# A constant moved ahead of the SBUF rings, and the output projections of four batches in a row in every second unit

## The chip, the cores and the metric

The kernel runs on one core of one Trainium2 chip, as one launch. The metric is device microseconds (us) of that core. The chip's engines have the names of the profile: PE (TensorE, the matmuls), PEld (its weight loads), DVE (VectorE), ACT (ScalarE), POOL (GpSimd) and SP (SyncE, which issues nearly all DMAs here).

## The reference

Four blocks change a residual `x` of 8 batches, 128 rows and 512 columns. Each adds tanh(gate) times its result to `x`; the first is by far the largest:

```python
x = x + tanh(g_xattn[0]) * L0_xattn(layernorm(x), ctx, mask, bias, ln_w, w_q, w_k, w_v, w_out)
x = x + tanh(g_ffn[0])   * L0_ffn(layernorm(x), 4-bit weights)
x = x + tanh(g_xattn[1]) * L1_xattn(layernorm(x), ctx, ...)
x = x + tanh(g_ffn[1])   * L1_ffn(layernorm(x), ...)
# L0_xattn: 32 heads of 128
score = einsum('bqhd,bkhd->bhqk', rmsnorm(x) @ w_q.T, ctx @ w_k.T) + position_bias
attn  = einsum('bhqk,bkhd->bqhd', softmax(masked score), ctx @ w_v.T)
out   = hidden + attn.reshape(b, q, 32 * 128) @ w_out.T
```

The last line is what the change touches: the projection of the heads' outputs, 4,096 wide, to 512 columns.

## The kernel before

**Number format.** Most products are made of three matmuls: each operand is split into a rounded high part and the low rest, and `product` (L172) adds high times high (L178), high times low (L179) and low times high (L182) in one PSUM bank. The operands have the type float32r, in which a column passes PE once; scores and attention (L691, L755) are plain float32, which the profile shows as two records for each matmul. A matmul has a stationary operand of 128 columns, loaded by PEld, and a moving one of up to 512 columns that streams past it.

**Stages.** First (to some 350 us) all keys and queries are projected and stored in DRAM. Then 64 *units* follow: unit u is one head and one half of the batches (four of them), four units to a pair of heads. At last (from some 740 us) the remaining projections and the other three blocks. In `unit(u)` (L1055) the program writes, in this order: output projections, steps of the value projection (`make_values`, in blocks of seven products that hold a PSUM bank `mm` over six of them), the attention of unit u-4 (`attend`, L743), another output projection, more value steps, the masks on POOL (`add_masks`), the scores of unit u with their softmax (`scores`, L683), then the loads, stores and the split of the next output weights (`split_wo`, L358).

**An output projection.** `project_out(p, b)` (L779) makes the 128 by 512 block `pso` of one batch b and one pair of heads p with six matmuls, three for each head: stationary are parts of the attention's output `a` (ring `page`), moving the parts `wo_h` and `wo_l` of the output weights (ring `wo`). After that one DVE instruction of L776 adds it times the gate to `xs[b]` and so frees its bank. A pair of heads has eight of these, n = 8p + b counts them all, 128 together. The PSUM ring `mm` has three banks, for `pso` and for the first accumulator `c1` of the value steps.

**Which unit takes which.** In unit u from 6 on, n = 2(u-6) is projected at the unit's beginning and n+1 after the attention. The last twelve are written out in `ending()` (L1406), two to four at a time.

**What sets the order.** The framework's planner orders the instructions of each engine when the program is built: it walks its own estimate of the time, prefers what is written earlier, and takes what is written later where the earlier isn't ready. It works on single instructions, so that six matmuls of a projection can be parted by those of a value step. `behind(name)` (L140) queues each instruction of a block, on the engine of the marked one, behind the instruction that has last been marked with that name; `mark` sets it. Within the units PE's order is the planner's, but for such edges; in the first and the last stage it is that of the program text (`in_order`).

**Where tiles lie.** SBUF tiles of the pool `sb` are laid out in the order in which their tags first occur, each rounded up to 32 bytes. The first 1,152 bytes are the framework's. Behind them stand the rings `raw` (7 tiles of 2,048 bytes) and `wo` (8), `pT` (2), the eight rows `xs`, `gates_in` (16 bytes, so 32), then the rings `moved` and `bias`, `ident`, `neghalf` (32 bytes, L411), small tiles, and the rings `v`, `page`, `kq` and `s`. So `raw`, `wo`, `pT` and `xs` begin at multiples of 64 bytes (`wo` at 15,488), and `moved`, `bias`, `ident`, `v`, `page`, `kq` and `s` at 32 bytes past such a multiple (`page` at 92,320).

Of the kernel before, what the change touches and what calls it, by code (L numbers as in the profile page):

```python
# [17 lines left out]
P = 128  # L18
NB = 8
# [47 lines left out]
def kernel(  # L67
# [37 lines left out]
    nc = tc.nc  # L105
# [6 lines left out]
    def keep(shape, name, dtype=F32):  # L112
        return sb.tile(shape, dtype, tag=name, name=name)
# [4 lines left out]
    def page(shape, name, dtype=F32R):  # L118


        return slot(shape, "page", name, dtype)

    def wide_row(tag, name, dtype=F32):
        return slot([P, D], tag, name, dtype)

    def ptile(shape, tag, name):
        return psum.tile(shape, F32, tag=tag, name=name, bufs=BANKS[tag])

    def wide(t):

        return t.bitcast(F32)
# [4 lines left out]
    def mark(name, inst):  # L136
        marks[name] = inst.ins

    @contextmanager
    def behind(*names):  # L140
        with ExitStack() as stack:
            for name in names:
                stack.enter_context(tc.issue_after(marks[name]))
            yield
# [27 lines left out]
    def product(out, terms, start=True, stop=True, **more):  # L172


        n = len(terms)
        for i, ((lh, ll), (rh, rl)) in enumerate(terms):
            first, last = start and i == 0, stop and i == n - 1
            nc.tensor.matmul(out, lhsT=lh, rhs=rh, start=first, stop=False, **more)  # L178
            nc.tensor.matmul(out, lhsT=lh, rhs=rl, start=False, stop=False, **more)  # L179
            mark(  # L180
                "product",
                nc.tensor.matmul(out, lhsT=ll, rhs=rh, start=False, stop=last, **more),  # L182
            )
# [191 lines left out]
    def load_half(h, inner):  # L375
        if inner == 0:
            raws[f"wk_{h}"] = slot([P, NDC, P], "raw", f"raw_wk_{h}")
        dcs = slice(inner * HK, inner * HK + HK)
        nc.sync.dma_start(out=raws[f"wk_{h}"][:, dcs], in_=wk[:, h, dcs])

    for inner in range(2):
        for half in range(2):
            for dc in range(inner * HK, inner * HK + HK):
                if half == 0 and dc == inner * HK:
                    load_half(0, inner)
                t = wide_row("wo", f"cxraw{half}{dc}")
                queue = nc.scalar if dc == half == 0 else nc.sync
                queue.dma_start(out=t, in_=ctxT[:, dc, half * HALF * P : (half + 1) * HALF * P])
                cx_raw[half, dc] = t
                if half == 0 and dc == inner * HK:  # L390
                    load_half(1, inner)
# [16 lines left out]
    idle = ptile([P, P], "av", "idle")  # L408
    for _ in range(WARMING):
        nc.tensor.matmul(idle, lhsT=ident, rhs=ident, start=True, stop=True)  # L410
    neghalf = keep([P, NB], "neghalf")  # L411
    nc.gpsimd.memset(neghalf, -0.5)

    tg = keep([P, 4], "tg")
# [217 lines left out]
    def by_block(t):  # L632

        return t.rearrange("p b (n k) -> p n b k", k=Q32)
# [31 lines left out]
    def where(u):  # L666

        p, r = divmod(u, 4)
        half, i = divmod(r, 2)
        return 2 * p + i, half  # L670

    def add_masks(u):

        h, half = where(u)
        s = slot([P, NQ, HALF, Q32], "s", f"s_{u}")
        bias = biases[h // 2][:, h % 2, :].rearrange("p (n k) -> p n k", k=Q32)
        with behind(*(f"norm{u - 2}",) * (u > 1)):
            nc.gpsimd.tensor_tensor(  # L678
                s, mneg[:, half], bias.unsqueeze(2).to_broadcast([P, NQ, HALF, Q32]), ALU.add
            )  # L680
        return s

    def scores(u, s):  # L683
        _, half = where(u)
        q, k = fetched.pop(("queries", u)), fetched.pop(("keys", u))
        bs = slice(half * HALF, (half + 1) * HALF)
        ps = ptile([P, HALF, P], "sc", f"sc_{u}")
        for j in range(HALF):
            cols = bass.ts(j, P)
            with behind(*("product",) * (u < SHORT)):  # L690
                nc.tensor.matmul(  # L691
                    ps[:, j, :], lhsT=q[:, cols], rhs=k[:, cols], start=True, stop=True
                )
        nc.vector.tensor_tensor(s, by_block(ps), s, ALU.add)  # L694
        nm = small.tile([P, HALF], F32, tag="nm", name=f"nm_{u}")
        mark(
            "max",
            nc.vector.tensor_reduce(  # L698
                nm, s.rearrange("p n b k -> p b n k"), AX.XY, ALU.max, negate=True
            ),  # L700
        )
        if u > 2:
            with behind("max"):
                transpose_probs(u - 3)
        sm = small.tile([P, HALF], F32, tag="sm", name=f"sm_{u}")
        for j in range(HALF):
            one = s[:, :, j, :]
            e = nc.scalar.activation(  # L708
                one, one, AF.Exp, bias=nm[:, j : j + 1], accum_out=sm[:, j : j + 1]
            )  # L710
        mark("exp", e)
        rs = small.tile([P, HALF], F32, tag="rs", name=f"rs_{u}")
        nc.vector.reciprocal(rs, sm)
        mark("rs", nc.vector.tensor_tensor(rs, rs, anykey[:, bs], ALU.mult))  # L714
        factors = rs.unsqueeze(1).unsqueeze(3).to_broadcast([P, NQ, HALF, Q32])
        mark(f"norm{u}", nc.gpsimd.tensor_tensor(s, s, factors, ALU.mult))  # L716
        probs[u] = s
# [19 lines left out]
    def transpose_probs(u):  # L737

        t = slot([P, HALF, P], "pT", f"pT_{u}")
        nc.vector.transpose(by_block(t), probs[u])  # L740
        probs[u] = t

    def attend(u):  # L743
        h, half = where(u)
        p, i = divmod(h, 2)
        pT = probs.pop(u)
        if i == 0:
            attns[p, half] = page([P, 2, 2, HALF, P], f"a_{p}_{half}")
        a = attns[p, half][:, i]
        ah, al = a[:, 0], a[:, 1]  # L750
        cols = bass.ts(i, P)
        av = ptile([P, HALF, P], "av", f"av_{u}")
        for b in range(HALF):
            v = values_of[p, half, b // 2][:, b % 2, :]
            nc.tensor.matmul(av[:, b, :], lhsT=v[:, cols], rhs=pT[:, b, :], start=True, stop=True)  # L755
        mark("a", nc.scalar.copy(ah, av))  # L756
        mark("al", nc.vector.tensor_tensor(al, av, wide(ah), ALU.subtract))  # L757

# [13 lines left out]
    def add_to_x(b, ps, factor, then=None):  # L772

        out = {} if then is None else {"accum_out": col(f"sum{then}", b)}
        mark(
            "x", nc.vector.scalar_tensor_tensor(xs[b], ps, factor, xs[b], ALU.mult, ALU.add, **out)  # L776
        )

    def project_out(p, b):  # L779
        half, j = divmod(b, HALF)  # L780
        ps = ptile([P, D], "mm", f"pso_{p}_{b}")
        product(
            ps,
            [
                (tuple(attns[p, half][:, i, part, j, :] for part in range(2)), wos[2 * p + i])
                for i in range(2)
            ],
        )
        add_to_x(b, ps, tgx0, "h1" if p == NP - 1 else None)
# [242 lines left out]
    def make_values(n):  # L1032
        nonlocal made
        while made < n:
            next(value_work, None)
            made += 1
# [18 lines left out]
    def unit(u):  # L1055
        p, r = divmod(u, 4)

        n = 2 * (u - OUT_LAG)

        goal = 14 + int(1.74 * (u - 3)) + min(AHEAD, u - 3, NU - 1 - u) if u > 3 else 0  # L1060
        if n >= 0:
            project_out(*divmod(n, NB))
        make_values((made + goal + 1) // 2)
        if u >= LAG:
            attend(u - LAG)
        if n >= 0:
            project_out(*divmod(n + 1, NB))
        make_values(goal)
        s = add_masks(u)
        for _ in range({0: 2, 1: 2, 2: 1, 3: 1, 4: 1}.get(u, 0)):  # L1070
            next(last_keys)
        scores(u, s)

        reads_first = 0 < u < SHORT or u == NU - 1
        if reads_first:
            move_probs(u - 1)
        with behind(*("moved",) * (0 < u < SHORT)):
            store_probs(u)
        if u and not reads_first:
            with behind("through"):  # L1080
                move_probs(u - 1)
        with behind("through" if u < SHORT else "moved"):
            loads(u + 1)
        if r < 2 and p:
            with behind("exp"):
                split_wo(2 * p - 2 + r)
        if u == NU - 1:
            with behind("exp"):
                split_wo(H - 2)

    make_values(7)
    unit(0)
    make_values(11)
    unit(1)
# [433 lines left out]
```

## Time and profile before

| | us |
|---|---|
| median of 3 runs (lowest to highest) | 911.24 (910.36 to 912.07) |
| the profiled execution's own time | 910.93 |
| its span, first to last instruction | 909.1 |
| PE busy in the span | 902.0 (99%) |
| DVE, ACT, POOL busy | 673.2 (74%), 503.1 (55%), 460.1 (51%) |
| granted PE clock | full |

A row of the profile's groups names the line, the engine, the operation, the tile written and those read, the shapes and how many there were; behind the bar stand the busy time in us, the mean duration of one in ns, and the engine's idle time just ahead of such instructions with what ended most of it. A row of the timeline gives the start and the duration in us of one instruction or of a few alike in a row. Matmuls overlap in the pipeline, so what a matmul takes of PE's time is read from one start to the next and not from its duration.

### The profile page before, as it was taken

What the parts mean: (1) busy time and instruction counts of PE and PEld (TensorE: products, weight loads), DVE (VectorE), ACT (ScalarE), POOL (GpSimd) and SP (SyncE); (2) the same over time, 40 slices, a digit from 0 to 9 for tenths busy, and PEclk for the clock granted to TensorE, in tenths of its full rate; (3) what the DMA queues carried; (4) which work ended last, traced back from release to release, by engine and by line L of the source; (5) the groups of instructions that cost most, each with busy time, mean ns of one, the idle gap of its engine ahead of it and who ended that gap; (6) DMA issues with size and microseconds to landing.
All of it is one profiled execution on the core that took longest, in us unless ns stands there. A gap on an engine that the chain in (4) does not pass through costs nothing.

```text
span 909.1 us, 16426 instructions
## 1 busy us (share of the span) xinstructions
PE 902.0 (99%) x5381; PEld 798.5 (88%) x5381; DVE 673.2 (74%) x1353; ACT 503.1 (55%) x1426; POOL 460.1 (51%) x513
## 2 busy tenths in 40 slices
PE   9999999999999999999999999999999999999998
PEld 7888888888888899999999999999999998888897
DVE  7888778788899866777677668666686877565587
ACT  6666565667555555544536345453554534587862
POOL 2355534124322436747748557583766844265441
PEclk9999999999999999999999999999999999999999
DMA  7754477889875956577484775766767566714001
GB/s 255 255 166 159 151 213 230 292 279 286 276 235 198 308 185 197 170 205 230 143 239 152 197 222 154 217 180 192 215 167 222 163 185 180 295 47 143 1 24 71
DMA packets 125222, 174.99 MB, mean 192 GB/s; under 512 B 17104, under 2 KB 54736, under 8 KB 124112
## 3 DMA queue, kind: packets, MB, share of 16 engines
q1 hardware_dynamic: 124992, 173.68, 61.0%
q8 instruction: 42, 0.69, 0.3%
q14 instruction: 44, 0.36, 0.1%
q10 hardware_dynamic: 144, 0.26, 0.1%
HBM read 109.86 MB, written 64.03 MB: 191 GB/s over the span
## 4 chain that ended last, share of the span: by engine, by line
PE 89%; DVE 3%; POOL 2%; DMA 2%; ACT 2%; issue 1%; SPq 0%; DVEq 0%; ACTq 0%; POOLq 0%
PE c_v L178 6%; PE c_v L182 6%; PE c_v L179 6%; PE pso L182 6%; PE pso L178 6%; PE sc L691 6%; PE pso L179 6%; PE av L755 6%; PE c_q L178 6%; PE c_q L179 6%; PE c_q L182 6%; PE c_k L178 4%; PE c_k L182 4%; PE c_k L179 4%; ACT h L1149 1%; DMA cxraw<-in_cxT_dram 1%
## 5 line engine op out<-in xcount | busy, mean ns | idle before, releaser
L708 ACT ACTIVATE s<-s,nm 128x128 f32<-128x128 f32 x256 | 99.8, 392 | 78.2 <-DVE nm L698 54.0
L776 DVE SCALAR_TENSOR_TENSOR x<-pso,tg,x 128x512 f32<-128x512 f32 x128 | 93.5, 741 | 53.7 <-PE pso L182 52.6
L716 POOL TENSOR_TENSOR s<-s,rs 128x512 f32<-128x512 f32 x64 | 66.7, 1042 | 111.2 <-DVE rs L714 58.5
L178 PE MATMUL pso<-wo_h,a 128*128 128x512 f32 x256 | 102.4, 413 | 0.0
L179 PE MATMUL pso<-wo_l,a 128*128 128x512 f32 x256 | 102.1, 399 | 0.0
L182 PE MATMUL pso<-wo_h,a 128*128 128x512 f32 x256 | 101.7, 397 | 0.1
L178 PE MATMUL c_v<-wvP,cxT 128*128 128x256 f32 x288 | 84.8, 294 | 0.1
L179 PE MATMUL c_v<-wvP,cxT 128*128 128x256 f32 x288 | 81.3, 282 | 0.0
L182 PE MATMUL c_v<-wvP,cxT 128*128 128x256 f32 x288 | 81.3, 282 | 0.0
L756 ACT CAST a<-av 128x512 fp32r<-128x512 f32 x64 | 37.3, 584 | 74.4 <-PE av L755 74.2
L678 POOL TENSOR_TENSOR s<-mneg,bias 128x512 f32<-128x512 bf16 x64 | 75.7, 1184 | 1.5 <-issue 1.2
L755 PE MATMUL av<-pT,v 128*128 128x128 f32 x512 | 71.2, 275 | 0.0
L755 PEld LDWEIGHTS av<-pT,v 128*128 128x128 f32 x512 | 67.2, 191 | 3.0
L691 PE MATMUL sc<-k,q 128*128 128x128 f32 x464 | 65.8, 274 | 0.0
L691 PEld LDWEIGHTS sc<-k,q 128*128 128x128 f32 x464 | 61.9, 191 | 3.4
L178 PE MATMUL c_v<-wvP,cxB 128*128 128x256 f32 x216 | 62.0, 289 | 0.0
L757 DVE TENSOR_TENSOR a<-av,a 128x512 fp32r<-128x512 f32 x64 | 43.4, 679 | 25.0 <-ACT a L756 24.8
L179 PE MATMUL c_v<-wvP,cxB 128*128 128x256 f32 x216 | 61.2, 283 | 0.0
L182 PE MATMUL c_v<-wvP,cxB 128*128 128x256 f32 x216 | 61.0, 282 | 0.0
L170 POOL TENSOR_TENSOR wo_l<-raw_wo,wo_h 128x512 fp32r<-128x512 f32 x32 | 41.3, 1292 | 34.3 <-ACT wo_h L169 34.3
L182 PEld LDWEIGHTS pso<-wo_h,a 128*128 128x128 f32 x256 | 48.2, 188 | 11.1 <-DVE a L757 1.3
L694 DVE TENSOR_TENSOR s<-sc,s 128x512 f32<-128x512 f32 x64 | 43.7, 684 | 17.7 <-PE sc L691 11.9
(277 smaller groups left out, 2805.9 us busy)
## 6 DMA issues: line engine op xcount, KB each, us to landing
keys<-keys SPq DMA_DIRECT2D x64, 256.0 KB, 3.3
queries<-queries SPq DMA_DIRECT2D x64, 256.0 KB, 3.6
through<-s SPq DMA_DIRECT2D x64, 256.0 KB, 3.3
moved<-through SPq DMA_DIRECT2D x256, 64.0 KB, 3.4
q<-queries SPq DMA_DIRECT2D x58, 256.0 KB, 3.9
k<-keys SPq DMA_DIRECT2D x58, 256.0 KB, 4.4
raw_wq<-in_wq_dram SPq DMA_DIRECT2D x32, 256.0 KB, 3.9
raw_wv<-in_wv_dram SPq DMA_DIRECT2D x32, 256.0 KB, 4.9
```

The source lines that it names most:

```text
L170: mark("low", (low_engine or nc.vector).tensor_tensor(low, src, wide(high), ALU.subtract))
L178: nc.tensor.matmul(out, lhsT=lh, rhs=rh, start=first, stop=False, **more)
L179: nc.tensor.matmul(out, lhsT=lh, rhs=rl, start=False, stop=False, **more)
L182: nc.tensor.matmul(out, lhsT=ll, rhs=rh, start=False, stop=last, **more),
L678: nc.gpsimd.tensor_tensor(s, mneg[:, half], bias.unsqueeze(2).to_broadcast([P, NQ, HALF, Q32]), ALU.add)
L691: nc.tensor.matmul(ps[:, j, :], lhsT=q[:, cols], rhs=k[:, cols], start=True, stop=True)
L694: nc.vector.tensor_tensor(s, by_block(ps), s, ALU.add)
L708: e = nc.scalar.activation(one, one, AF.Exp, bias=nm[:, j : j + 1], accum_out=sm[:, j : j + 1])
L716: mark(f"norm{u}", nc.gpsimd.tensor_tensor(s, s, factors, ALU.mult))
L755: nc.tensor.matmul(av[:, b, :], lhsT=v[:, cols], rhs=pT[:, b, :], start=True, stop=True)
L757: mark("al", nc.vector.tensor_tensor(al, av, wide(ah), ALU.subtract))
L776: "x", nc.vector.scalar_tensor_tensor(xs[b], ps, factor, xs[b], ALU.mult, ALU.add, **out)
```

## The change

Three edits:

- `neghalf`, a constant of 32 bytes, is allocated before the first ring and not behind `ident`. What lay ahead of its old place moves up by 32 bytes: `raw`, `wo`, `pT`, `xs` and `gates_in` then begin 32 bytes past a multiple of 64, and `moved`, `bias` and `ident` at a multiple of 64. Tiles behind the old place stay where they were. Its `memset` stays where it was.
- The two output projections of a unit are no longer parted. In units with n = 2, 6, 10, ... (u = 7, 9, ..., 63) the projections n-2 to n+1, four batches of one half and one pair of heads, are written at the unit's beginning, and none in the other units. The last twelve stay in `ending()`.
- The first of the four is queued on PE behind the last product, the last score matmul and the last attention matmul that were written before it. Two marks are added for that.

```diff
+    neghalf = keep([P, NB], "neghalf")
     for inner in range(2):
         for half in range(2):
             for dc in range(inner * HK, inner * HK + HK):
...
-    neghalf = keep([P, NB], "neghalf")
     nc.gpsimd.memset(neghalf, -0.5)
...
-                nc.tensor.matmul(
+                score = nc.tensor.matmul(
                     ps[:, j, :], lhsT=q[:, cols], rhs=k[:, cols], start=True, stop=True
                 )
+        mark("score", score)
...
-            nc.tensor.matmul(av[:, b, :], lhsT=v[:, cols], rhs=pT[:, b, :], start=True, stop=True)
+            one = nc.tensor.matmul(
+                av[:, b, :], lhsT=v[:, cols], rhs=pT[:, b, :], start=True, stop=True
+            )
+        mark("attended", one)
...
-        if n >= 0:
-            project_out(*divmod(n, NB))
+        if n >= 0 and n % 4 == 2:
+            with behind("product", "score", "attended"):
+                project_out(*divmod(n - 2, NB))
+            for j in range(n - 1, n + 2):
+                project_out(*divmod(j, NB))
         make_values((made + goal + 1) // 2)
         if u >= LAG:
             attend(u - LAG)
-        if n >= 0:
-            project_out(*divmod(n + 1, NB))
         make_values(goal)
```

## The prediction

> **What bounds the kernel now.** I read the page's busy shares first, then its groups, then the waits of PE, then PE's timeline, start to start.
>
> ```profile
> span 909.1 us, 16426 instructions
> PE 902.0 (99%) x5381; PEld 798.5 (88%) x5381; DVE 673.2 (74%) x1353; ACT 503.1 (55%) x1426; POOL 460.1 (51%) x513
> L178 PE MATMUL pso<-wo_h,a 128*128 128x512 f32 x256 | 102.4, 413 | 0.0
> L776 DVE SCALAR_TENSOR_TENSOR x<-pso,tg,x 128x512 f32<-128x512 f32 x128 | 93.5, 741 | 53.7 <-PE pso L182 52.6
> PE psq L182 <- DVE h2T L170: 0.3, 1, 0.3
> ```
>
> PE is the bound, and it waits for almost nothing: the view of its waits adds up to 3.2 us, and none of it lies in the units. A reordering can therefore win only what the matmuls themselves lose, and lose whatever new wait it makes. The second group is DVE's addition to `xs`, 741 ns, which frees a projection's bank; today DVE waits for it, never PE.
>
> What do the matmuls lose? The start of a matmul to the start of the next, all of 512 columns at the full clock, from three stretches of PE's timeline: a projection of outputs, one of queries, and one of the second block's queries.
>
> ```profile
> 793.22 0.40 PE L178 MATMUL pso<-wo_h,a 128*128 128x512 f32 x1
> ...
> 797.18 0.40 PE L182 MATMUL pso<-wo_h,a 128*128 128x512 f32 x1
> 797.42 0.60 PE L1126 MATMUL tph<-ident,h 128*128 128x128 f32 x4
> ```
>
> ```profile
> 249.83 0.39 PE L178 MATMUL c_q<-xqB,wqP 128*128 128x512 f32 x1
> ...
> 252.55 0.39 PE L178 MATMUL c_q<-xqT,wqP 128*128 128x512 f32 x1
> ```
>
> ```profile
> 822.16 0.39 PE L179 MATMUL psq<-wq,h2T 128*128 128x512 f32 x1
> ...
> 823.32 0.39 PE L178 MATMUL psq<-wq,h2T 128*128 128x512 f32 x1
> ...
> 824.68 0.60 PE L1126 MATMUL tpk<-ident,k 128*128 128x128 f32 x4
> ```
>
> The output projection takes 4.20 us for 18 matmuls, 233.3 ns each, and stays there to the end of a run of 24. The query projection takes 2.72 us for 12: 226.7 ns. `psq` shows both: five matmuls in 1.16 us (232.0 ns) behind other work, then six in 1.36 us (226.7 ns). So a 512-column run begins near 232 and settles at 227 after some six matmuls, but the runs of `pso` never settle. By the layout, the moving operands of `c_q` and `psq` lie in `page`, 32 bytes past a multiple of 64, as do all the stationary ones; that of `pso` alone lies in `wo`, at a multiple of 64.
>
> **The change part by part.** The sum is made against the profiled execution's own 910.93 us, 0.31 us under the median of the runs.
>
> *The 32 bytes.* They add no instruction. `wo` comes to stand as `page` does, and I take it that `pso` then settles as `psq`. The ends: nothing (no row shows `wo` at another place, so its distance from `page`, not its phase, may be the cause), and 768 matmuls x 6.6 ns = 5.1 us if all ran at 226.7 from the first. For runs of six, as most are today, little comes of it: they are over before they settle. The first six of a run cost 232 in either layout.
>
> *The four in a row.* The 768 matmuls and 128 additions remain. Units 7, 9, ..., 63 make 29 groups of 24 matmuls; 72 matmuls stay in the ending, already in long runs. In a settled run of 24, the first six take 6 x 232 = 1,392 ns and the other 18 x 226.7 = 4,081, together 5.47 us; today 24 take, in runs of six to twelve, 24 x 232.7 = 5.58. (232.7 is between the 232.0 of a beginning and the 233.3 of a long run.) That is 0.11 us a group, 29 x 0.11 = 3.2 us. The ending's runs (two of 24, two of 12) have 48 matmuls past their sixth: 48 x 6.6 ns = 0.3 us. Together 3.5 us. A switch from value matmuls to `pso` costs nothing more to speak of: the first `pso` is some 4 ns longer (567.34 to 567.58 in the timeline), the first value matmul behind one some 3 ns shorter, so the switches saved are worth 0 to 0.1 us.
>
> If the planner parts a group in two runs of twelve (it does so wherever a bank isn't free by its own time), each settles anew: 29 x 6 x 5.3 ns = 0.9 us of the gain goes.
>
> *The later projection and its edge.* Two of each four are written one unit later, the other two in their old unit; the weights' split (L170 on POOL, 1,292 ns) thus gains a unit for the first two. The page of `a` and the slots of `wo` were already held for the later two, so no load on SP and no split on POOL starts later; no DMA is moved. The edge holds the first of the four behind scores and attention of the unit before. Both are written before it anyway; what it takes away is that the planner may draw a projection forward as filler. In the units PE's idle time is nil today; I book nothing, and with the cover gone it is the second rival's price.
>
> *The bank.* Two `mm` banks are left for `pso` while `c1` lives. The third projection then needs the first one's addition done. The timeline of DVE and PE gives the best case: the last matmul of a projection starts, 0.43 us later its addition starts and takes 0.75, together 1.18; the second projection occupies PE for 0.23 + 6 x 0.232 = 1.62 us from the same point. That leaves 0.44 us. But the group now stands right behind the scores, whose own additions come first on DVE:
>
> ```profile
> 475.69 0.69 DVE L694 TENSOR_TENSOR s<-sc,s 128x512 f32<-128x512 f32 x1 [1.09 <-issue]
> 476.42 0.69 DVE L698 TENSOR_REDUCE nm<-s 128x4 f32<-128x512 f32 x1
> 477.02 0.70 DVE L740 STREAM_TRANSPOSE pT<-moved 128x512 f32<-128x512 f32 x1
> 477.87 0.75 DVE L776 SCALAR_TENSOR_TENSOR x<-pso,tg,x 128x512 f32<-128x512 f32 x1
> ```
>
> These three take 2.0 us from the scores' end (about 0.4 us into the group) to 2.4; then the addition ends at 3.1, while PE would be free at 2.8: 0.3 us late. Ends: nothing, where the planner puts value matmuls in the gap or `c1` doesn't live, and 29 x 0.3 = 8.7 us, where nothing fits. I take a tenth, 0.9 us, nearest to the row of today, since the planner already filled such gaps in every unit and PE's waits show none on DVE there.
>
> *Other tiles that shift.* `xs`, `raw` and `pT` go to 32 past 64, `ident`, `moved` and `bias` to a multiple of it. All their users are off the path, or matmuls of 128 columns that take 0.11 us for each load of weights in whatever ring they lie (`av` with `pT` at a multiple of 64 and `sc` with `kq` past it: 1.06 us for eight records both). DVE, idle for a quarter, hides a change of some per cent in L776; if all 128 became 10% longer, those of the last eight batches alone would show, under 0.6 us. Nothing booked; 0.6 either way kept for the range.
>
> Sum: -3.5 + 0.9 = -2.6 us: 908.3 for a profiled execution, 908.6 for the median.
>
> **The rivals.**
>
> *The phase isn't the cause.* `pso` stays at 233 in any run, and the change only moves work: 910.9 and at most 0.9 more, 911.2 to 912.1 as a median. For it speaks that ring and phase can't be told apart in this trace; against it, that `page` beside `page` (`psq`) and `page` beside `v` (`c_q`) settle alike, so the ring seems not to matter. [...] A variant: `wo` settles but the planner parts the groups into sixes, 1 us gained, 910.2. Chance of the two, no change: 0.25.
>
> *Slower: the crowded DVE.* The third projection waits 0.3 us in nearly every group and nothing fills it, since `c1` of the next value step waits for the same banks: +8.7 - 3.5 = +5.2, 916.4; with no gain from the phase, 919.9. It decides from 3.5 / 29 = 0.12 us a group on. For it: DVE has 2.0 us of softmax and 4 x 0.75 of additions in a group of 5.6 us, nearly 90%; units without projections are only about 4.3 us of PE's work, in which POOL's two passes (1,184 and 1,042 ns) and the splits must keep up. Against it: the planner fills gaps single matmul by single matmul (its runs today are of 1 to 12), and over two units every engine has the load it had. Chance 0.23.
>
> **How the numbers follow.** Forecast, faster by some 2.6 us: 0.52. About 0.2% (1.8 us) is what a measurement of this kernel can tell from no change. Faster 0.52, same 0.25, slower 0.23. The likeliest case's own range is 906.9 (all that can settle does, no wait: -3.5, and the 0.6 and a little for the runs' spread) to 909.4. The range for all goes from 906.6 up into the slower rival, to 915.5, leaving out its worst half and the most favourable twentieth.
>
> **What would show it.** In the changed kernel's timeline a run of `pso` should reach 226 to 227 ns from its seventh matmul on, and the mean durations of the three `pso` groups should fall from 397 to 413 toward the 389 of `c_q`. The runs should be of 24 in every second unit. PE's waits should show no more than about 1 us on L776. A rate of 233 in long runs shows the first rival; PE idle ahead of L178, ended by DVE's `x`, the second. I would be wrong altogether if the order on POOL or ACT, which I can't see before it is planned, starved the attention in the short units.

## The result, and the profile after

The changed kernel takes 909.05 us (median of 18 runs, 908.00 to 910.25), the kernel before 911.21 (18 runs, 909.76 to 912.14): a ratio of 0.998, 95% interval 0.9974 to 0.9987, so 1.2 to 2.4 us less. The forecast was 908.6.

Of the page of the changed kernel, the span, the busy shares, and the groups that answer to those of before:

```profile
span 907.5 us, 16407 instructions
PE 900.6 (99%) x5381; PEld 799.4 (88%) x5381; DVE 675.1 (74%) x1353; ACT 503.5 (55%) x1426; POOL 458.9 (51%) x513
L781 DVE SCALAR_TENSOR_TENSOR x<-pso,tg,x 128x512 f32<-128x512 f32 x128 | 93.2, 740 | 35.4 <-PE pso L182 34.8
L178 PE MATMUL pso<-wo_h,a 128*128 128x512 f32 x256 | 103.2, 411 | 0.0
L182 PE MATMUL pso<-wo_h,a 128*128 128x512 f32 x256 | 100.7, 393 | 0.1
L179 PE MATMUL pso<-wo_l,a 128*128 128x512 f32 x256 | 100.5, 392 | 0.0
```

PE is still busy for 99%, and its waits still hold nothing from the units: those behind 340 us that the list names, 0.2 to 0.3 us each, stand in the last stage, and the only new one is at 779 us.

```profile
PE c_v L178 <- ACT v L253: 0.2, 1, 0.2
```

The span is 1.6 us shorter. The mean durations of L182 and L179 have gone from 397 and 399 ns to 393 and 392. Two matmuls of one run in PE's timeline, the seventh and the last, and what follows:

```profile
425.13 0.39 PE L178 MATMUL pso<-wo_h,a 128*128 128x512 f32 x1
...
426.26 0.39 PE L182 MATMUL pso<-wo_h,a 128*128 128x512 f32 x1
426.49 0.72 PE L757 MATMUL av<-pT,v 128*128 128x128 f32 x5
```

From 425.13 to 426.49 us stand six matmuls in 1.36 us, 226.7 ns each; the kernel before needs 233.3 in its long runs. So the output projection settles now, as `psq` did.

The runs on PE are mostly not of 24, though: 32 runs are of 12, 31 of six, 2 of 24 (both in the ending) and 22 of another length, 13 of these of two to five. No group of the units is one run: of the 29, nine came as two runs of 12, three as 18 and six, and seventeen in three to five pieces.

For the comparisons below, PE's time is split by adding up the distances from the start of each matmul to the start of the next, over one profiled execution of each kernel. "First six" and "later" are mean distances (ns) of the `pso` matmuls among the first six of their run and behind them, without distances of 260 ns and over (a switch from a plain float32 matmul, 314 to 318 ns in the changed kernel's runs of 12, or a wait). Scores and attention are given beside `pso`, as some of a switch's time is booked on the one or the other by what follows what.

| kernel | `wo` / `page` past a multiple of 128 bytes | first six | later | `pso` us | scores + attention us | value us |
|---|---|---|---|---|---|---|
| before | 0 / 32 | 232.7 | 233.5 | 185.6 | 109.4 | 186.2 |
| changed | 32 / 32 | 231.1 | 228.5 | 182.7 | 110.2 | 186.7 |
| shift alone | 32 / 32 | 231.4 | 227.7 | 184.0 | 109.4 | 186.6 |
| four alone | 0 / 32 | 232.7 | 233.3 | 184.8 | 110.2 | 186.3 |
| shift of 64 | 64 / 32 | 232.8 | 233.3 | 185.0 | 110.2 | 187.3 |
| all at 64 | 0 / 0 | 231.1 | 228.5 | 182.8 | 110.0 | 186.6 |
| page apart | 32 / 64 | 232.8 | 233.3 | 185.1 | 110.1 | 187.0 |
| shift of 96 | 96 / 32 | 231.3 | 229.8 | 183.3 | 110.2 | 186.6 |

### The profile page after: what moved, and what is told of

It reads as the page before. It is cut to its first block, busy times and chain, and to the rows that moved or that the text cites. A ratio compares the mean times of both kernels' runs of the same rounds, so it can differ in the third digit from the quotient of the medians.

```text
span 907.5 us, 16407 instructions
## 1 busy us (share of the span) xinstructions
PE 900.6 (99%) x5381; PEld 799.4 (88%) x5381; DVE 675.1 (74%) x1353; ACT 503.5 (55%) x1426; POOL 458.9 (51%) x513
## 4 chain that ended last, share of the span: by engine, by line
PE 89%; POOL 2%; DVE 2%; ACT 2%; DMA 2%; issue 1%; SPq 0%; DVEq 0%; ACTq 0%; POOLq 0%
PE c_v L178 7%; PE c_v L179 6%; PE c_v L182 6%; PE sc L692 6%; PE pso L182 6%; PE pso L178 6%; PE av L757 6%; PE pso L179 6%; PE c_q L178 6%; PE c_q L179 6%; PE c_q L182 6%; PE c_k L178 4%; PE c_k L179 4%; PE c_k L182 4%; ACT h L1155 1%; DMA cxraw<-in_cxT_dram 1%
## 5 line engine op out<-in xcount | busy, mean ns | idle before, releaser
L182 PE MATMUL pso<-wo_h,a 128*128 128x512 f32 x256 | 100.7, 393 | 0.1
L179 PE MATMUL pso<-wo_l,a 128*128 128x512 f32 x256 | 100.5, 392 | 0.0
L179 PE MATMUL c_v<-wvP,cxT 128*128 128x256 f32 x288 | 81.6, 283 | 0.0
L182 PE MATMUL c_v<-wvP,cxT 128*128 128x256 f32 x288 | 81.4, 283 | 0.0
L692 PE MATMUL sc<-k,q 128*128 128x128 f32 x464 | 63.0, 275 | 0.0
L179 PE MATMUL c_v<-wvP,cxB 128*128 128x256 f32 x216 | 61.4, 284 | 0.0
L182 PE MATMUL c_v<-wvP,cxB 128*128 128x256 f32 x216 | 61.3, 285 | 0.0
L692 PEld LDWEIGHTS sc<-k,q 128*128 128x128 f32 x464 | 58.7, 191 | 1.2
L182 PEld LDWEIGHTS pso<-wo_h,a 128*128 128x128 f32 x256 | 48.1, 188 | 11.8 <-DVE a L762 1.3
L178 PEld LDWEIGHTS c_v<-wvP,cxT 128*128 128x128 f32 x288 | 54.9, 191 | 1.5 <-ACT v L253 0.4
```

Source lines behind the costliest of these rows:

```text
L692: score = nc.tensor.matmul(ps[:, j, :], lhsT=q[:, cols], rhs=k[:, cols], start=True, stop=True)
```

## The experiments

The theory (P): a run of 512-column matmuls settles at 227 ns where moving and stationary operand lie at the same place within 64 bytes, and stays at 233 where they are 32 bytes apart. Against it stood that the order alone wins (S), that some other distance does it (D), that a moving operand at a multiple of 64 is slow by itself (A), and that the output projection alone is sensitive, by its ring (R). Each ratio is to the kernel before on the same chip.

### The shift alone, and the four alone

The shift alone is the kernel before with the first hunk of the diff:

```diff
+    neghalf = keep([P, NB], "neghalf")
     for inner in range(2):
...
-    neghalf = keep([P, NB], "neghalf")
     nc.gpsimd.memset(neghalf, -0.5)
```

> The 32 bytes alone, projections as before. Theory P (a run of 512-column matmuls settles at 227 ns only where moving and stationary operand lie at the same place within 64 bytes): runs of pso settle, but most are of six and over before that; positions two to six of a run fall from about 232.4 to 230.8 ns (what the changed kernel shows in its runs), 600 matmuls x 1.6 ns = 1.0 us, about 910.2. Rival S (the order alone wins, by fewer switches between kinds of matmul): 911.2, and pso at 233 ns.

Measured: 908.92 against 910.49 us, ratio 0.9983 (0.9974 to 0.9992). The operands of the attention (`pT`, `v`) change their places to each other too, but scores and attention stay at 109.4 us; only `pso` gets shorter. The four alone is the changed kernel without that hunk:

```diff
-    neghalf = keep([P, NB], "neghalf")
     for inner in range(2):
...
+    neghalf = keep([P, NB], "neghalf")
     nc.gpsimd.memset(neghalf, -0.5)
```

> The four projections in a row alone, rings where they were. Theory P: pso alternates 235 and 232 ns through every run, no gain: 911.2, give or take 0.6. Rival S: all of the gain is here, 909.1.

Measured: 910.48 against 910.49 us, ratio 1.0001 (0.9992 to 1.001). The planned order of PE in each is exactly that of the kernel from which it has its order, so only the addresses differ. S falls: the order alone brings nothing. In the table `pso` seems 0.8 us shorter with the four alone, but scores and attention are 0.8 longer; together they are the same as before. The 32 bytes alone bring 1.6 us, more than the 1.0 that was expected.

### Which place: 64 bytes on, everything at 64, page apart

Three kernels have the changed kernel's order of matmuls and other addresses. The first puts another 32 bytes ahead of the rings:

```diff
+    rcs = keep([P, NB], "rcs")
     neghalf = keep([P, NB], "neghalf")
...
-    rcs = keep([P, NB], "rcs")
     fnw_p, knw, qnw = (keep([P, NDC], n) for n in ("fnw_p", "knw", "qnw"))
```

> The changed kernel with 64 bytes ahead of the rings (a second constant of 32 bytes, rcs, is allocated there too), so that wo stands at a multiple of 64 again, but 64 bytes further. Theory P: like the four alone, 911.2, pso at 233 ns. Rival D (any other distance of wo from page does it, not the place within 64 bytes): 909.1, pso settles at 227.

Measured: 911.20 us, ratio 1.0007 (0.9998 to 1.0016): no gain, so D falls as it was put. From PE's timeline, the seventh matmul of a run and what follows its twelfth:

```profile
424.54 0.40 PE L178 MATMUL pso<-wo_h,a 128*128 128x512 f32 x1
...
425.71 0.39 PE L182 MATMUL pso<-wo_h,a 128*128 128x512 f32 x1
425.94 0.49 PE L758 MATMUL av<-pT,v 128*128 128x128 f32 x3
```

Six in 1.40 us, 233 ns. The second leaves the front as before and moves `v` and `page` instead:

```diff
-    neghalf = keep([P, NB], "neghalf")
     for inner in range(2):
...
+    neghalf = keep([P, NB], "neghalf")
     nc.gpsimd.memset(neghalf, -0.5)
...
-    rcs = keep([P, NB], "rcs")
     fnw_p, knw, qnw = (keep([P, NDC], n) for n in ("fnw_p", "knw", "qnw"))
...
     of_context = next(making)
+    rcs = keep([P, NB], "rcs")
     of_rows = query_operands()
```

> The four in a row, with wo at a multiple of 64 as before, but v and page moved there too (rcs is allocated behind them). Theory P: moving and stationary at the same place again, pso settles at 227 and the projections of keys and queries stay there: 909.1. Rival A (a moving operand at a multiple of 64 is slow by itself): pso stays at 233, and the 1,356 matmuls of keys and queries, whose moving operand is in page, go from 227 to 233 as well, 1,356 x 6.6 ns = 8.9 us more: about 920.

Measured: 908.15 us, ratio 0.9975 (0.9966 to 0.9983). The same two rows:

```profile
424.17 0.39 PE L178 MATMUL pso<-wo_h,a 128*128 128x512 f32 x1
...
425.31 0.39 PE L182 MATMUL pso<-wo_h,a 128*128 128x512 f32 x1
425.54 0.83 PE L757 MATMUL av<-pT,v 128*128 128x128 f32 x6
```

Six in 1.37 us, 228 ns, with `wo` at the very addresses of before. A falls: no place is slow by itself. It is the two operands' places against each other.

The third takes the changed kernel and moves `page`, and what lies behind it, away from `v` and `wo`:

```diff
+    qkn = keep([P, NDC], "qkn")
     making = context_operands()
...
-    qkn = keep([P, NDC], "qkn")
```

> The changed kernel with page alone (and what lies behind it) moved by 32 bytes, to a multiple of 64; wo and v stay 32 past it. Moving and stationary operand are then apart in all projections of keys and queries (moving page, stationary v) and in pso (moving wo, stationary page, the other way round than before). Theory P: the 1,356 matmuls of keys and queries go from 227 to 233 ns, 8.9 us more, and pso goes back to 233, 2.9 more: about 921. Rival R (only the output projection's operands are sensitive, by their ring): keys and queries stay at 227, about 909 to 912.

Measured: 918.26 (median of four runs) against 910.43 us, ratio 1.0083 (1.0068 to 1.0099). A query projection in its timeline, twelve matmuls:

```profile
254.92 0.39 PE L178 MATMUL c_q<-xqT,wqP 128*128 128x512 f32 x1
...
257.72 0.39 PE L178 MATMUL c_q<-xqT,wqP 128*128 128x512 f32 x1
```

2.80 us for twelve, 233.3 ns, where the kernel before needs 2.72. R falls: the rate follows the operands' places in another stage and other rings too, and `pso` is back at 233.3. The expectation says that `wo` and `page` are then apart the other way round than before. By the addresses they aren't: `wo` is at 15,520 and `page` at 92,352, so `page` is 32 bytes ahead within 128, as before. It is in the queries (moving operand at 64, stationary at 32 past a multiple of 128) and in the shift of 64 that the moving operand is ahead. The queries' 672 matmuls take 156.8 us instead of 152.7, 6.1 ns each. If all 1,356 matmuls of both projections lose as much, that makes 8.3 us, and `pso` is 2.4 longer than in the changed kernel: 10.7 together, in a profile of the slowest of the four runs (920.99 us). The measured difference of the medians is 9.9 (7.8 over the kernel before, and that kernel 2.1 over the changed one); 11.8 had been expected.

### How far apart: 96 bytes

All of this fits 128 bytes as well as 64. A shift of 96 puts `wo` and `page` alike within 64 bytes, but 64 apart within 128:

```diff
+    rcs = keep([P, NB], "rcs")
+    fnw_p = keep([P, NDC], "fnw_p")
     neghalf = keep([P, NB], "neghalf")
...
-    rcs = keep([P, NB], "rcs")
-    fnw_p, knw, qnw = (keep([P, NDC], n) for n in ("fnw_p", "knw", "qnw"))
+    knw, qnw = (keep([P, NDC], n) for n in ("knw", "qnw"))
```

> The changed kernel with 96 bytes ahead of the rings (two more small constants stand there), so that wo and page stand alike within 64 bytes, but 64 apart within 128. Theory P with 64 bytes: pso settles at 227 and the time is that of the changed kernel, 2.1 us under the kernel before. Theory P with 128 bytes, which all runs so far allow as well: pso stays at 233, and the time is that of the kernel before.

Measured: 909.17 against 910.33 us, ratio 0.9988 (0.9978 to 0.9997), between the two expectations. So are the matmuls: most runs cycle through 226, 229 and 232 ns, a few stay at 233 to 234 throughout, 229.8 on average behind the sixth. Both forms of P fall in their plain shape: 64 bytes apart is better than 32 and worse than the same place.

### What the order is worth

Two in a row at the beginning of each unit, in place of four in every second:

```diff
-        if n >= 0 and n % 4 == 2:
+        if n >= 0:
             with behind("product", "score", "attended"):
-                project_out(*divmod(n - 2, NB))
-            for j in range(n - 1, n + 2):
-                project_out(*divmod(j, NB))
+                project_out(*divmod(n, NB))
+            project_out(*divmod(n + 1, NB))
```

> The 32 bytes, and two projections in a row at the beginning of every unit instead of four in every second. By the planned order, 62 runs are of six and 17 of 12 or more, as with the shift alone. Theory P: no better than the shift alone, 1.6 us under the kernel before, pso some 184.0 us from start to start. Rival (that the two are written one behind the other is what counts, not the length of the runs on PE): 2.2 us under, as the changed kernel.

Measured: 911.45 against 910.43 us, ratio 1.002 (1.0009 to 1.0032), slower than either expectation, though `pso` has the 184.4 us that P asks for. Its runs spread from 910.58 to 915.46 us. The profile, of the 910.58 us run, shows three new gaps. One is at 705.7, where attention follows a projection and waited for its transposed probabilities:

```profile
705.70 0.39 PE L182 MATMUL pso<-wo_h,a 128*128 128x512 f32 x1
706.01 0.71 DVE L742 STREAM_TRANSPOSE pT<-moved 128x512 f32<-128x512 f32 x1 [2.04 <-DMA moved<-through]
706.84 0.52 PEld L757 LDWEIGHTS av<-pT,v 128*128 128x128 f32 x4 [1.18 <-PE pso L182]
706.87 0.57 PE L757 MATMUL av<-pT,v 128*128 128x128 f32 x3 [0.79 <-DVE pT L742]
```

The transpose itself had waited for the DMA that moves the probabilities. The second, at 565.7, is 0.6 us ahead of the scores. These two make 1.6 us over what such matmuls take; the third, at 349.9, is 0.3 us ahead of value matmuls. Together they cancel the shift's gain; what the slower runs add wasn't profiled. The same two in a row without the edge wasn't run, so it is argued, not shown, that the edge makes these gaps.

The changed kernel without its edge:

```diff
-            with behind("product", "score", "attended"):
-                project_out(*divmod(n - 2, NB))
-            for j in range(n - 1, n + 2):
+            for j in range(n - 2, n + 2):
                 project_out(*divmod(j, NB))
```

> The changed kernel without the edge behind product, scores and attention: the planner may draw the first projection of the four forward. In the planned order 571 of the 768 matmuls stand among the first six of their run, against 490 in the changed kernel and 634 with the shift alone. Theory P: the time goes by that count, some 4.5 ns each: 0.4 us above the changed kernel, 0.3 under the shift alone. Rival E (the edge is a burden, as it was in every unit): as fast as the changed kernel or faster.

Beside it, on the same chip, the changed kernel and the shift alone once more:

> The changed kernel itself, beside the shift alone on one chip. Theory P: 2.2 us under the kernel before and 0.6 us under the shift alone, for 144 fewer matmuls among the first six of a run. Rival: the four in a row bring nothing, and both are the same.

> The shift alone once more, for the comparison: 1.6 us under the kernel before, and 0.6 us over the changed kernel.

Measured, against 910.76 us: the changed kernel 908.76 (0.9977, interval 0.9968 to 0.9986), without the edge 909.10 (0.9981, 0.9972 to 0.9990), the shift alone 909.25 (0.9983, 0.9974 to 0.9992). The medians stand in the order, and nearly at the distances, that the count of matmuls among the first six gives, but the intervals overlap by more than the steps. That the four in a row add some 0.5 us to the shift is likely and not settled, and neither is rival E.

At last every matmul of the unit queued behind the four:

```diff
             for j in range(n - 1, n + 2):
-                project_out(*divmod(j, NB))
-        make_values((made + goal + 1) // 2)
...
+                with behind("product"):
+                    project_out(*divmod(j, NB))
+        with behind(*("product",) * (n >= 0 and n % 4 == 2)):
+            make_values((made + goal + 1) // 2)
...
```

(The block goes on to the unit's `scores`.)

> The changed kernel with every matmul of the unit queued behind the four projections, so that 25 groups are single runs of 24 (in the changed kernel most are two of 12 with scores or attention between). Theory P: 270 or so fewer matmuls stand among the first six of a run, at 231 instead of 227 ns, 1.1 us less: 908.0 against 909.1 of the changed kernel, if PE doesn't wait. Rival W (the planner parts the groups because the third projection's bank isn't free, DVE being crowded): PE idle ahead of L178, ended by x, 0.3 us in each of 29 groups, 8.7 us: 917.

Measured: 927.26 (median of four runs) against 910.43 us, ratio 1.0191 (1.0177 to 1.0206). The profile is of the slowest of them, 930.42 us, and its span is 21.1 us longer than the changed kernel's. PE's waits, line by line what was waited for, the us in total, how often, and the longest:

```profile
PE pso L179 <- POOL wo_l L170: 9.2, 9, 2.6
PE idle L412 <- POOL ident masks.py:199: 1.4, 1, 1.4
PE av L757 <- DVE pT L742: 1.4, 3, 0.7
```

and those of its weight loads that concern `x`:

```profile
PEld pso L178 <- DVE x L781: 3.4, 13, 0.3
```

W has the sign right, less than half of the size, and the wrong cause. PE waits for POOL's split of the output weights, above all. In the changed kernel attention, scores and value matmuls stand at that place (363.3 to 366.3 us in the first group, between its two heads). The bank that DVE frees, W's cause, holds the loads of the weights back 13 times for 0.3 us at most; in the starts of the matmuls these 13 places cost some 1.5 us.

The two longest waits cost more than themselves. Behind them, 2.6 us up to 365.6 and 2.5 us up to 714.6, the matmuls start 427 ns apart for some microseconds, and come back to 230:

```profile
365.57 0.50 PE L179 MATMUL pso<-wo_l,a 128*128 128x512 f32 x1 [2.58 <-POOL wo_l L170]
...
366.72 0.63 PE L179 MATMUL pso<-wo_l,a 128*128 128x512 f32 x1
367.15 0.63 PE L182 MATMUL pso<-wo_h,a 128*128 128x512 f32 x1
...
369.56 0.40 PE L182 MATMUL pso<-wo_h,a 128*128 128x512 f32 x1
369.79 0.40 PE L178 MATMUL pso<-wo_h,a 128*128 128x512 f32 x1
```

From 366 to 369 us the granted clock is 0.50; the mean over the execution is 0.996, against 1.000 in the changed kernel's. By the starts of the matmuls the two slow stretches lose some 2.9 us. With the waits for POOL (9.2) and for the transposed probabilities (1.4) and the bank (1.5) that explains 15 of the 21.1 us; the rest wasn't followed up.

## Why the prediction was right, and which terms were off

- *PE is the bound and loses only in its own matmuls*: borne out; in the changed kernel there is no wait in the units after either.
- *The 32 bytes let `pso` settle*: shown, by the shift alone, by the loss of the gain at 64, and by moving the other operand. The first rival falls: by it the shift would have changed nothing, and it was worth 1.6 us. That `pso` settles was right (226.7 ns, and 228.5 on average behind the sixth); the sizes by which it becomes time were not, as the next two points say.
- *Little comes of it for runs of six*: mis-sized. The shift alone has some three quarters of the whole gain. The first six of a run also fell, from 232.7 to 231.4 ns, where I had 232 in either layout: 558 x 1.3 = 0.7 us. And the 134 matmuls that stood behind a sixth even in the old order fell by 5.8 ns: 0.8 us.
- *29 groups of 24*: mis-sized. I counted 29 x 18 + 48 = 570 matmuls behind a sixth; there are 278, since no group of the units came whole. Behind the sixth the mean is 228.5 and not 226.7, as a run of twelve has hardly settled. So of the 3.5 us, these matmuls brought some 1.3: 134 that fell by 5.0 ns and 144 that fell by 4.2. The variant of two runs of twelve, priced at 0.9 us less, was too mild.
- *The bank, 0.9 us*: the wait isn't there in the changed kernel. Two kernels with the same order show one such wait each, 0.5 us (64 bytes) and 0.4 us (page apart). That the planner parts the group because of the bank is argued: runs mostly end after one or two whole projections, which fits the two free banks. If so, I charged as a wait what appears as parted runs. Forced, it costs some 1.5 us, not the 8.7 of the upper end.
- *Switches at 0 to 0.1 us*: not seen as a gain. The value matmuls became 0.5 us longer; with the shift alone, whose order is that of before, 0.4 in one profile and 0.2 in the other; but without the edge, with the same places, they take 186.2 us as before. Where it comes from stays open.
- *The sum*: of the predicted 3.5 us gain, `pso` with scores and attention show 2.2 (295.1 to 292.9), less 0.5 of the value matmuls: 1.7 between the two profiles, whose spans differ by 1.6. The predicted net, 2.6, was somewhat too large; the medians differ by 2.2. That it came so near is luck in part: the long runs brought some 2.1 us less than booked, and two misses the other way, 0.9 for a wait that isn't there and 0.7 from the first six (424 x 1.6 ns), made up for most of it.
- *The edge at nothing*: no wait shows for one in every second unit, and with and without it the medians are 0.3 us apart, less than the intervals can tell. The price that I named for lost filler shows with everything queued behind the four; that it is also the price of the edge in every unit (two in a row) is argued.

## What to carry to other kernels

Read matmuls from start to start, stage by stage: a steady 3% between two stages of equal shape (233.3 against 226.7 ns) is worth an explanation, and here it stood in the profile of before. Where PE is the bound and its matmuls are like these, lay the rings of moving and of stationary operands so that the addresses differ by a multiple of 512 bytes, as in all runs here that settle at 227 ns (32 bytes apart they stay at 233); a small constant moved in the allocation does it. Leave the planner its filler: an edge that keeps a block of matmuls whole can take away what covers another engine's lateness, as queuing everything behind the four did (9.2 us of waits for POOL).

## What the hardware showed that was not expected

- The rate of the 512-column float32r matmuls goes by where the two operands lie against each other: at the same place, 227 ns once settled (227.7 and 228.5 on average behind the sixth); 64 bytes apart, 229.8 on average; 32 apart, 233.3, whichever operand is ahead. Places are counted within 128 bytes here, but in every run that settles they are alike within 512 (`page` stands 76,800 bytes, 150 x 512, behind the shifted `wo`, and tiles and their parts are multiples of 512 long). Whether 128 or 256 apart would do as well was not tried, nor were distances that aren't multiples of 32. Why the place counts is not shown.
- A run that can settle takes three to ten matmuls to do so in the changed kernel, by a sequence that repeats to a nanosecond or two (229, 233, 236, 224, 231, 236, 228, 233, 231, 226, ...); one that can't alternates between 235 and 232 to its last matmul, in the kernel before to the end of a run of 24.
- The trace of before held a second, weaker witness: the 328-column `o` matmuls of the last block, whose two halves lie 32 bytes apart (within 64) in one tile. Those with the moving part at a multiple of 64, stationary 32 past one, took 150.6 ns (without the switches), the others 149.1. That fits, but no run moves these two operands against each other.
- Two waits of PE, of 2.5 and 2.6 us (with everything queued behind the four), were each followed by a stretch at half the granted clock, in which 512-column matmuls started 427 ns apart. With the page apart such matmuls also start 427 ns apart from 5.91 to 10.17 us, behind a wait of 0.57 us, where the mean clock of the execution is 1.000; so what brings the slow stretches is not shown.
